# Rotary partners from swapped weight columns, centred value weights, and every fourth head's exponentials from PSUM

## The chip, the cores and the metric

The kernel runs on one core of a Trainium2 chip. Its time is the device time of one execution in microseconds. Three runs of the kernel before the change gave a median of 19321.17 us (19318.22 to 19327.21). The core has five engines that run side by side, each working through its own list of instructions in order: PE (matrix products, which land in PSUM), DVE (elementwise operations and reductions), ACT (tabulated functions and copies), POOL, and SP, which here only starts DMA transfers. An engine that reaches an instruction whose input isn't ready stands still, and everything behind that instruction waits too.

## What is computed

Thirty-two audio signals of 160,000 samples become 32 sequences of 313 frames of 512 samples. Then, cut to what matters:

```python
h = frames @ dct.T                                   # 313 x 512 per sequence
# attention on layernorm(h): 8 heads of width 64
Q = xpos(X @ W_Q); K = xpos(X @ W_K); V = X @ W_V    # xpos: x*cos + rot(x)*sin
#   rot(x)[2i] = -x[2i+1];  rot(x)[2i+1] = x[2i]
p = softmax(Q @ K.T) * gamma_h ** abs(n - m)
Y = p @ V
Yn = (Y - mean(Y)) * rsqrt(var(Y) + 1e-5)            # per head, over its 64 columns
h = h + (silu(X @ W_G) * (Yn * gn_weight + gn_bias)) @ W_O
# feed-forward on x = layernorm(h), 256 neurons
theta = x[..., None, :] / (1 + abs(W)) + B           # 512 angles for each neuron and frame
s, c = sin, cos of theta, rounded to 4096 steps of the circle
out = sum(c * attn_cos) @ proj_cos.T + sum(s * attn_sin) @ proj_sin.T
h = h + silu(out)
```

The sines are the bulk of it: for each neuron, ACT evaluates one sine and one cosine of every element of every frame.

## The kernel before

**Work and stages.** Sequences are taken in eight groups of four (a "quad"). `attention` handles one sequence at a time: DCT, layernorm, projections, heads, norm, output projection. `ffn` handles a quad at once, one neuron after another; its data lie with the 512 features over 4 x 128 partitions and 4 x 313 frames along the free dimension. For each neuron DVE makes the index of the sine (four affine operations at L556, a mask at L563), then the index of the cosine (L568, L574); ACT evaluates both (L581, 5008 elements a partition each, into one of three `trig` buffers); PE sums them over features with a table of weights, `hot` (L591). There are two pairs of index buffers, so DVE can run about one neuron ahead of ACT.

The first quad's attention runs before any FFN work, two sequences side by side in two sets of buffers, A and B; each has its own PSUM tile W of four banks. After that only set A is left, and the attention of the next quad is laid between the neurons of the current one. The eighth quad's FFN has no attention beside it.

**What sets the order.** Nothing is issued as the Python code runs. Each operation is added to a `Plan` with a key (when it is due, in half neurons), an engine, an estimated duration, and what it reads and writes; PSUM is named by bank there (`banks`). `emit` simulates the engines with these durations: each engine takes the ready operation with the lowest key, and the instructions are issued in that order. The chip then runs every engine's list in exactly this order, with semaphores between engines that the tile framework derives from the tiles themselves.

**The lines that the change touches.** `rows` and `columns` load weights of 256 KB into a ring of three buffers (`load`, L203) and multiply: `rows` gives three row blocks in banks 0 to 2 (L274), `columns` one block of 128 output columns in one bank with four matmuls (L288). For each pair of heads g (L326 to L345), two column blocks give q and k in banks 0 and 1; ACT copies both to `raw` (L209); DVE multiplies them by the cosine table (L334); PE multiplies `raw` by a constant matrix `rot`, which swaps neighbours and sets signs, into banks 2 and 3 (L339); DVE multiplies by the sine table (L343) and adds (L344). For each head, PE makes the scores in banks 0 to 2 (L353), DVE takes each row's maximum (L361) and writes scores minus maximum to `prob` (L364). After four heads, ACT takes their exponentials in place, one call per head and row block, with row sums (L372), between two changes of its table. For each of the four heads, PE transposes (L390), DVE multiplies by the decay (L402), and PE multiplies by the values (L408) into bank 3. After every second head DVE takes the mean of each head's 64 columns (L424, L425) and writes the difference to `xn` (L429). The norm follows (L439 to L459), with the square on ACT and the inverse square root on POOL.

Of the kernel before, what the change touches and what calls it, by code (L numbers as in the profile page):

```python
# [12 lines left out]
F32 = mybir.dt.float32  # L13
I32 = mybir.dt.int32
I16 = mybir.dt.int16
AF = mybir.ActivationFunctionType
# [110 lines left out]
def tile_audio_tower(ctx: ExitStack, tc: tile.TileContext, t: dict, out: bass.AP):  # L127
# [20 lines left out]

    xT_d = dram.tile([P, NC4, T], F32, name="xT_d")
    sums_d = dram.tile([2, P, 2, T], F32, name="sums_d")  # L150
    h_d = dram.tile([n_quads, QUAD, S, HOP], F32, name="h_d")

    class Buffers:


        def __init__(self, name, pool, psum):
            self.name = name
            self.n_ring = 0

# [12 lines left out]
            self.raw = sb("raw", 2, S)  # L172
            self.prob = sb("prob", NB, NT, S)
            self.probT = sb("probT", NT, S)
            wide = self.prob.rearrange("p a b s -> p (a b s)")
            self.sq = wide[:, : NT * HOP].rearrange("p (i d) -> p i d", d=HOP)
            self.hres = self.sq
            self.aff = wide[:, NT * HOP : NT * HOP + NC4 * S].rearrange("p (c s) -> p c s", s=S)
            self.mx = [sb(f"mx{i}", NT) for i in range(2)]
            for key in ("sm", "gm", "gv", "gr", "gu"):  # L180
                setattr(self, key, sb(key, NT, H))
            self.st = sb("st", NT, nc.vector.BN_STATS_DIM)
            self.mv = sb("mv", NT, 2)
            for key in ("lv", "lr", "lu"):
                setattr(self, key, sb(key, NT))
            self.W = psum.tile([P, 4, 512], F32, name=f"{name}_W")

            self.y = self.W[:, 3, : NT * 2 * DH].rearrange("p (i d) -> p i d", d=2 * DH)
# [7 lines left out]
        def every(self, key, n):  # L196
            return [self.k(key, x) for x in range(n)]

        def load(self, plan, key, src):

            i = self.n_ring % N_RING
            self.n_ring += 1
            plan.add(key, "SP", DMA_NS, lambda: nc.sync.dma_start(self.ring[i], src), (),  # L203
                     (self.k("ring", i),))
            return i

    def copy(plan, key, eng, n, dst, src, r, w):
        if eng == "ACT":
            plan.add(key, eng, 220 + 0.833 * n, lambda: nc.scalar.copy(dst, src), r, w)  # L209
        else:  # L210
            plan.add(key, eng, 160 + 1.042 * n, lambda: nc.vector.tensor_copy(dst, src), r, w)
# [52 lines left out]
                    )  # L264
            plan.add(key, "PE", 800, go, x.every("xn", NT), x.banks(c))

    def rows(plan, key, x, lhsT, src, r, order=range(NT)):

        for c in range(NC4):
            k = x.load(plan, key, src[c])  # L270
# [21 lines left out]
    def attention(plan, keys, q, b, x):  # L292
# [4 lines left out]
        def step(n=1.0):  # L297
            done[0] += n
            return keys(done[0] / 139.0)
# [9 lines left out]
        copy(plan, step(), ENG_XNT, NC4 * S, x.xnT, x.W[:, :, :S], x.banks(0, 1, 2, 3), (x.k("xnT"),))  # L309


        rows(plan, step(7), x, x.xnT, t["wv"], (x.k("xnT"),), range(NT - 1, -1, -1))
        copy(plan, step(), ENG_V, NT * HOP, x.v[:N], W3, x.banks(0, 1, 2), (x.k("v"),))
        plan.add(step(0), "POOL", 500, lambda: nc.gpsimd.memset(x.v[0:1, : NT - 1, :], 0.0), (),
                 (x.k("v"),))
# [9 lines left out]
        for hb in range(H // NB):  # L325
            for g in range(hb * NB // 2, (hb + 1) * NB // 2):  # L326
                key = step(4)
                qk = x.qk[g % 2]
                kq = x.k("qk", g % 2)
                columns(plan, key, x, 0, t["wq"][g])  # L330
                columns(plan, key, x, 1, t["wk"][g])
                copy(plan, key, "ACT", 2 * S, x.raw, x.W[:, 0:2, :S], x.banks(0, 1), (x.k("raw"),))
                plan.add(key, "DVE", 810,
                         lambda qk=qk: nc.vector.tensor_tensor(qk, x.W[:, 0:2, :S], cos_qk, ALU.mult),  # L334
                         x.banks(0, 1), (kq,))

                def go():
                    for i in range(2):
                        nc.tensor.matmul(x.W[:, 2 + i, :S], rot, x.raw[:, i, :], start=True, stop=True)  # L339
                plan.add(key, "PE", 1100, go, (x.k("raw"),), x.banks(2, 3))  # L340

                def turned(qk=qk):
                    nc.vector.tensor_tensor(x.raw, x.W[:, 2:4, :S], sin_qk, ALU.mult)  # L343
                    nc.vector.tensor_tensor(qk, qk, x.raw, ALU.add)  # L344
                plan.add(key, "DVE", 1640, turned, x.banks(2, 3), (x.k("raw"), kq))  # L345
            for hd in range(hb * NB, (hb + 1) * NB):
# [3 lines left out]
                for i in range(NT):  # L350
# [9 lines left out]
                plan.add(key, "DVE", 1150,  # L360
                         lambda m=m: nc.vector.tensor_reduce(m[:N], x.W[:N, :NT, :S], AX.X, ALU.max),  # L361
                         x.banks(0, 1, 2), (x.k("mx", hd % 2),))
                plan.add(key, "DVE", 1150,
                         lambda m=m, a=a: nc.vector.tensor_tensor(  # L364
                             x.prob[:N, a], x.W[:N, :NT, :S],
                             m[:N].unsqueeze(2).to_broadcast((N, NT, S)), ALU.subtract),
                         (x.k("mx", hd % 2), *x.banks(0, 1, 2)), (x.k("prob", a),))

            def exps(hb=hb):
                for a in range(NB):  # L370
                    for i in range(NT):
                        nc.scalar.activation(  # L372
                            x.prob[:N, a, i, :], x.prob[:N, a, i, :], AF.Exp,
                            accum_out=x.sm[:N, i, hb * NB + a : hb * NB + a + 1],
                        )

                nc.scalar.activation(x.lu[:1, 0:1], x.lu[:1, 0:1], AF.Silu)
            plan.add(step(), "ACT", 8700, exps, (), [*probs, x.k("sm", hb), x.k("lu")])
            for hd in range(hb * NB, (hb + 1) * NB):
                key = step(5)  # L380
                a, d = hd % NB, hd % 2
# [33 lines left out]
                if hd % 2 == 0:  # L415
                    continue

                key = step()
                h0 = hd - 1
                y4 = x.y[:N].rearrange("p i (h e) -> p i h e", e=DH)  # L420
                m = x.gm[:N, :, h0 : h0 + 2]

                def means(m=m, y4=y4):
                    nc.vector.tensor_reduce(m, y4, AX.X, ALU.add)  # L424
                    nc.vector.tensor_scalar(m, m, 1.0 / DH, None, ALU.mult)  # L425
                plan.add(key, "DVE", 750, means, x.banks(3), (x.k("gm", h0),))
                plan.add(
                    key, "DVE", 560,
                    lambda h0=h0, m=m, y4=y4: nc.vector.tensor_tensor(  # L429
                        x.xn[:N, :, h0 * DH : (h0 + 2) * DH].rearrange("p i (h e) -> p i h e", e=DH),  # L430
                        y4, m.unsqueeze(3).to_broadcast((N, NT, 2, DH)), ALU.subtract),
                    (*x.banks(3), x.k("gm", h0)), xns,
                )


# [182 lines left out]
        nc.sync.dma_start(tl, t[key])  # L618
        return tl

    rot = load("rot", P)
    cos_qk = load("cos_qk", 2, S)
    sin_qk = load("sin_qk", 2, S)
    gnw = load("gnw", NC4)
# [4 lines left out]
    def affine(plan, key, x):  # L629
# [11 lines left out]
        def go():  # L641
# [11 lines left out]
        plan.add(key, "DVE", 14000, go, (), ["f", *x.every("prob", NB)])  # L653

    SLOTS = 2.0 * NF
    plan = Plan()
    A = Buffers("a", const, psum)
    affine(plan, -2000.0, A)
# [1 line left out]
    inner = ExitStack()  # L660
    B = Buffers("b", inner.enter_context(tc.tile_pool(name="early", bufs=1)),
                inner.enter_context(tc.tile_pool(name="early_psum", bufs=1, space=PSUM)))
    for b in range(QUAD):
        attention(plan, lambda x: -1000.0 + b // 2 + x, 0, b, (A, B)[b % 2])

# [22 lines left out]
def _constants(S):  # L688
# [18 lines left out]
    for fn, val in (("sin", sin), ("cos", cos)):  # L707
        both = []
        for z in (zeta, (f(1.0) / zeta).astype(f)):
            r = np.repeat(val * z, 2, axis=-1).T  # L710
            both.append(np.concatenate([r, r], 0))
        c[f"{fn}_qk"] = np.ascontiguousarray(np.stack(both, 1))

    rot = np.zeros((P, P), f)
    even = np.arange(0, P, 2)
    rot[even + 1, even] = -1.0
    rot[even, even + 1] = 1.0
    c["rot"] = rot

    lo, hi = f(math.log(1.0 / 32)), f(math.log(1.0 / 512))  # L720
    step = np.arange(H, dtype=f) / f(H - 1)
# [29 lines left out]
def _layout(x, W_Q, W_K, W_V, W_G, W_O, gn_weight, gn_bias, W, B_param, attn_cos, attn_sin, pc, psn):  # L751
# [6 lines left out]
    def heads(w):  # L758
        return w.transpose(1, 0, 2).reshape(HOP, H * DH)

    a["wq"], a["wk"], a["wg"] = _columns(heads(W_Q)), _columns(heads(W_K)), _columns(W_G)
    a["wv"], a["wo"] = _rows(heads(W_V)), _rows(W_O)
    a["gnw"] = np.ascontiguousarray(gn_weight.reshape(NC4, P).T)
    a["gnb"] = np.ascontiguousarray(gn_bias.reshape(NC4, P).T)
# [37 lines left out]
```

## Time and profile before

| | |
|---|---|
| median of three runs | 19321.17 us (19318.22 to 19327.21) |
| the profiled execution | 19307.72 us |
| its span, first to last instruction | 19305.9 us |
| ACT busy | 18394.0 us (95%) |
| DVE busy | 17893.9 us (93%) |
| PE busy (matmuls) | 14624.3 us (76%) |
| POOL busy | 583.0 us (3%) |
| first sine on ACT | 619.3 us after the start |
| one cycle of a quad, FFN and attention | 2348.4 us |

All times below are microseconds unless marked ns. A line of a group gives the source line, engine, operation, output and inputs, shape and count, then busy time, mean ns of one, and the engine's idle time just before with what ended it. Busy times of a group leave out overlap of neighbours, so they can be below count times mean. An engine's idle time costs only where that engine, at that moment, sets the pace.

### The profile page before, as it was taken

Reading aid. Unit: us, or ns where it says so; the run is one execution under the profiler, and the core shown is the slowest. Engines: PE = TensorE matmul, PEld = TensorE weight load, DVE = VectorE, ACT = ScalarE, POOL = GpSimd, SP = SyncE. Lnnn points to the kernel's source line nnn. Section 1 sums busy time; section 2 is a strip of 40 time slices with the busy share of each in tenths; the row PEclk is TensorE's granted clock in tenths of the full one; section 3 lists DMA queues with packets and bytes.
Section 4 is the critical chain, followed back from the end, with each engine's and each line's share of the span. In section 5 each row is a group of like instructions: output and inputs, shape, how many; then the busy total and the mean of one; then the engine's idle time right before and its main releaser. Section 6 shows DMA issues by size and latency. Waiting matters only on the chain.

```text
span 19305.9 us, 332892 instructions
## 1 busy us (share of the span) xinstructions
PE 14624.3 (76%) x147328; PEld 6443.6 (33%) x147328; DVE 17893.9 (93%) x17258; ACT 18394.0 (95%) x6179; POOL 583.0 (3%) x1222
## 2 busy tenths in 40 slices
PE   8777778777787777777777777777777777766666
PEld 5333333333333333333333333233333333322222
DVE  4899999999999999999999999999999999999997
ACT  1799999999999999999999999999999999999998
POOL 0000000000000000000000000000000000000000
PEclk7899989999899998999989999899998999999988
DMA  2111111111111111111111111111111111110001
GB/s 81 41 36 38 36 31 59 37 37 37 35 53 39 36 37 46 43 38 37 37 57 31 36 37 38 56 37 34 35 38 60 35 36 36 36 48 17 18 18 36
DMA packets 418068, 759.10 MB, mean 39 GB/s; under 512 B 50000, under 2 KB 99280, under 8 KB 416624
## 3 DMA queue, kind: packets, MB, share of 16 engines
q1 hardware_dynamic: 416624, 737.80, 12.6%
q8 instruction: 1156, 18.94, 0.4%
q14 instruction: 288, 2.36, 0.0%
HBM read 655.55 MB, written 82.05 MB: 38 GB/s over the span
## 4 chain that ended last, share of the span: by engine, by line
DVE 37%; ACT 34%; PE 15%; issue 11%; POOL 2%; DMA 0%; DVEq 0%; ACTq 0%; SPq 0%; POOLq 0%
ACT trig L581 32%; DVE ix L556 14%; PE pa L591 9%; DVE ix L563 6%; DVE ix L568 6%; DVE ix L574 5%; PE a_W L274 2%; PE a_W L288 1%; DVE a_prob L364 1%; DVE a_mx L361 1%; ACT a_prob L372 1%; PE a_W L353 0%; POOL a_lu L225 0%; PE a_W L408 0%; DVE a_st L237 0%
## 5 line engine op out<-in xcount | busy, mean ns | idle before, releaser
L581 ACT ACTIVATE trig<-ix 128x5008 f32<-128x5008 int16 x4096 | 17539.1, 4366 | 280.2 <-DVE ix L563 202.5
L591 PE MATMUL pa<-trig,hot 128*32 128x313 f32 x131072 | 10641.9, 471 | 4110.8 <-ACT trig L581 4089.2
L591 PEld LDWEIGHTS pa<-trig,hot 128*32 128x32 f32 x131072 | 4127.4, 117 | 10249.9 <-ACT trig L581 5925.4
L556 DVE TENSOR_SCALAR ix<-xT,f_scale,f_bias 128x1252 int16<-128x1252 f32 x8192 | 7099.1, 927 | 273.3 <-ACT trig L581 266.7
L568 DVE TENSOR_SCALAR ix<-ix 128x5008 int16<-128x5008 int16 x2048 | 3005.6, 1468 | 202.2 <-ACT trig L581 16.1
L574 DVE TENSOR_SCALAR ix<-ix 128x5008 int16<-128x5008 int16 x2048 | 3004.6, 1467 | 63.8
L563 DVE TENSOR_SCALAR ix<-ix 128x5008 int16<-128x5008 int16 x2048 | 2998.7, 1464 | 67.3
L288 PE MATMUL a_W<-a_xnT,a_ring 128*128 128x313 f32 x2880 | 834.2, 435 | 0.0
L274 PE MATMUL a_W<-a_ring,a_a 128*105 128x512 f32 x1488 | 696.8, 609 | 24.4 <-DMA a_ring<-in_dct 12.9
L353 PE MATMUL a_W<-a_qk 64*105 64x313 f32 x1440 | 522.3, 482 | 232.6 <-DVE a_prob L364 182.7
L288 PEld LDWEIGHTS a_W<-a_xnT,a_ring 128*128 128x128 f32 x2880 | 529.0, 190 | 282.5 <-issue 72.9
L408 PEld LDWEIGHTS a_W<-a_v,a_probT 105*105 105x105 f32 x4320 | 484.1, 189 | 277.4 <-issue 212.2
L408 PE MATMUL a_W<-a_v,a_probT 105*105 105x64 f32 x4320 | 547.9, 278 | 11.3 <-DVE a_probT L402 8.3
L274 PE MATMUL a_W<-a_ring,a_gate 128*105 128x512 f32 x720 | 370.3, 633 | 62.5 <-DVE a_gate L471 62.5
L353 PEld LDWEIGHTS a_W<-a_qk 64*105 64x105 f32 x1440 | 226.9, 179 | 524.0 <-DVE a_prob L364 270.7
L274 PEld LDWEIGHTS a_W<-a_ring,a_a 128*105 128x105 f32 x1488 | 240.4, 173 | 416.7 <-issue 384.4
L372 ACT ACTIVATE a_prob<-a_prob 105x313 f32<-105x313 f32 x720 | 322.9, 450 | 52.6 <-DVE a_prob L364 52.0
L225 POOL TENSOR_TENSOR a_gu<-a_gr 105x24 f32<-105x24 f32 x90 | 48.7, 541 | 10254.2 <-DVE a_gr L219 10249.5
L274 PE MATMUL a_W<-a_ring,a_xnT 128*105 128x512 f32 x720 | 351.5, 612 | 3.1 <-ACT a_xnT L209 3.1
L261 PE MATMUL a_W<-ident,a_xn 105*128 105x105 f32 x1080 | 185.4, 301 | 189.4 <-DVE a_xn L249 96.0
L390 PE MATMUL a_W<-ident,a_prob 105*105 105x105 f32 x2160 | 321.6, 283 | 8.2 <-DVE a_xn L429 5.3
L361 DVE TENSOR_REDUCE a_mx<-a_W 105x3 f32<-105x939 f32 x240 | 271.0, 1129 | 41.0 <-PE a_W L353 40.9
(137 smaller groups left out, 4368.2 us busy)
## 6 DMA issues: line engine op xcount, KB each, us to landing
hot<-in_hot SPq DMA_DIRECT2D x1024, 256.0 KB
a_dec<-in_decay SPq DMA_DIRECT2D x240, 260.5 KB
a_ring<-in_proj SPq DMA_DIRECT2D x128, 256.0 KB
a_ring<-in_dct SPq DMA_DIRECT2D x120, 256.0 KB
a_ring<-in_wv SPq DMA_DIRECT2D x120, 256.0 KB
a_ring<-in_wg SPq DMA_DIRECT2D x120, 256.0 KB
a_ring<-in_wq SPq DMA_DIRECT2D x120, 256.0 KB
a_ring<-in_wk SPq DMA_DIRECT2D x120, 256.0 KB
```

The source lines that it names most:

```text
L274: lambda c=c, i=i, k=k, to=to: nc.tensor.matmul(x.W[:N, to, :], lhsT[:, c, ROW0[i] : ROW0[i] + N], x.ring[k], start=(c == 0), stop=(c == N ...
L288: nc.tensor.matmul(x.W[:, bank, :S], w[:, c, :], x.xnT[:, c, :], start=(c == 0), stop=(c == NC4 - 1))
L353: lambda i=i, qk=qk, r0=r0: nc.tensor.matmul(x.W[:N, i, :S], qk[r0 : r0 + DH, 0, ROW0[i] : ROW0[i] + N], qk[r0 : r0 + DH, 1, :], start=Tru ...
L361: lambda m=m: nc.vector.tensor_reduce(m[:N], x.W[:N, :NT, :S], AX.X, ALU.max),
L372: nc.scalar.activation(x.prob[:N, a, i, :], x.prob[:N, a, i, :], AF.Exp, accum_out=x.sm[:N, i, hb * NB + a : hb * NB + a + 1],)
L408: nc.tensor.matmul(x.y[:N, i, (hd % 2) * DH : (hd % 2 + 1) * DH], x.probT[:N, jj, ROW0[i] : ROW0[i] + N], x.v[:N, jj, hd * DH : (hd + 1) * ...
L556: nc.vector.tensor_scalar(now["ix", x][:, c, :], now["xT", c], f_scale[:, c, n : n + 1], f_bias[:, c, n : n + 1], ALU.mult, ALU.add)
L563: nc.vector.tensor_scalar(now["ix", x], now["ix", x], LUT - 1, LUT // 2, ALU.bitwise_and, ALU.bitwise_xor)
L568: nc.vector.tensor_scalar(new("ix", y, [P, NC4, T], I16, bufs=N_IX), now["ix", x], float(LUT // 4), None, ALU.add)
L574: nc.vector.tensor_scalar(now["ix", x], now["ix", x], LUT - 1, None, ALU.bitwise_and)
L581: nc.scalar.activation(new("trig", w, [P, NC4, T], bufs=N_TRIG), now["ix", x], AF.Sin, bias=-PI32, scale=ANG)
L591: nc.tensor.matmul(now["pa", p][b * 32 : b * 32 + 32, :S], now["hot", z][:, n % 2, c, k, :], now["trig", w][:, c, b * S : (b + 1) * S], st ...
```

## The change

Four edits. The rotary partners of q and k come from two more column blocks, with weights whose neighbouring columns are swapped (`wq_s`, `wk_s`, prepared with the other weights); the sign moves into the sine table, and the copy to `raw` and the matrix `rot` go. A new function `centre` runs once at the start: it loads the value weights into B's `prob`, subtracts from each head's 64 columns their mean, and stores the result in DRAM as `wv_d`, which every sequence then loads in place of `wv`; the values, and so the head outputs, have zero mean, and the mean on DVE goes. For the last head of every four, DVE no longer writes scores minus maximum: it negates the maximum, and ACT's exponential reads the scores from PSUM with the negated maximum as its bias. The tile `gm` goes.

```diff
+    wv_d = dram.tile([NC4, P, HOP], F32, name="wv_d")
...
-        rows(plan, step(7), x, x.xnT, t["wv"], (x.k("xnT"),), range(NT - 1, -1, -1))
+        rows(plan, step(7), x, x.xnT, wv_d, (x.k("xnT"),), range(NT - 1, -1, -1),
+             ("wv_d",))
...
                 columns(plan, key, x, 0, t["wq"][g])
                 columns(plan, key, x, 1, t["wk"][g])
-                copy(plan, key, "ACT", 2 * S, x.raw, x.W[:, 0:2, :S], x.banks(0, 1), (x.k("raw"),))
+                columns(plan, key, x, 2, t["wq_s"][g])
+                columns(plan, key, x, 3, t["wk_s"][g])
...
-                def go():
-                    for i in range(2):
-                        nc.tensor.matmul(x.W[:, 2 + i, :S], rot, x.raw[:, i, :], start=True, stop=True)
-                plan.add(key, "PE", 1100, go, (x.k("raw"),), x.banks(2, 3))
...
+                if a == NB - 1:
+                    plan.add(key, "DVE", 100,
+                             lambda m=m: nc.vector.tensor_scalar(m[:N], m[:N], -1.0, None, ALU.mult),
+                             (), (x.k("mx", hd % 2),))
+                    continue
...
-            def exps(hb=hb):
+            def exps(hb=hb, m=m):
                 for a in range(NB):
                     for i in range(NT):
+                        last = a == NB - 1
                         nc.scalar.activation(
-                            x.prob[:N, a, i, :], x.prob[:N, a, i, :], AF.Exp,
+                            x.prob[:N, a, i, :],
+                            x.W[:N, i, :S] if last else x.prob[:N, a, i, :], AF.Exp,
+                            bias=m[:N, i : i + 1] if last else 0.0,
                             accum_out=x.sm[:N, i, hb * NB + a : hb * NB + a + 1],
                         )
...
-            plan.add(step(), "ACT", 8700, exps, (), [*probs, x.k("sm", hb), x.k("lu")])
+            plan.add(step(), "ACT", 8700, exps, (x.k("mx", 1), *x.banks(0, 1, 2)),
+                     [*probs, x.k("sm", hb), x.k("lu")])
...
-                def means(m=m, y4=y4):
-                    nc.vector.tensor_reduce(m, y4, AX.X, ALU.add)
-                    nc.vector.tensor_scalar(m, m, 1.0 / DH, None, ALU.mult)
-                plan.add(key, "DVE", 750, means, x.banks(3), (x.k("gm", h0),))
                 plan.add(
-                    key, "DVE", 560,
-                    lambda h0=h0, m=m, y4=y4: nc.vector.tensor_tensor(
-                        x.xn[:N, :, h0 * DH : (h0 + 2) * DH].rearrange("p i (h e) -> p i h e", e=DH),
-                        y4, m.unsqueeze(3).to_broadcast((N, NT, 2, DH)), ALU.subtract),
-                    (*x.banks(3), x.k("gm", h0)), xns,
+                    step(), "DVE", 560,
+                    lambda h0=h0: nc.vector.tensor_copy(
+                        x.xn[:N, :, h0 * DH : (h0 + 2) * DH], x.y[:N]),
+                    x.banks(3), xns,
                 )
...
-    rot = load("rot", P)
...
+    def centre(plan, key, x):
+        wide = x.prob.rearrange("p a b s -> p (a b s)")
+        w = wide[:, : NC4 * HOP].rearrange("p (c d) -> p c d", d=HOP)
+        w3 = wide[:, : NC4 * HOP].rearrange("p (n e) -> p n e", e=DH)
+        m = wide[:, NC4 * HOP : NC4 * HOP + NC4 * H]
+        probs = x.every("prob", NB)
+        def fetch():
+            for c in range(NC4):
+                nc.sync.dma_start(w[:, c, :], t["wv"][c])
+        plan.add(key, "SP", NC4 * DMA_NS, fetch, (), probs)
+        def go():
+            nc.vector.tensor_reduce(m, w3, AX.X, ALU.add)
+            nc.vector.tensor_scalar(m, m, 1.0 / DH, None, ALU.mult)
+            nc.vector.tensor_tensor(
+                w3, w3, m.unsqueeze(2).to_broadcast((P, NC4 * H, DH)), ALU.subtract)
+        plan.add(key, "DVE", 5000, go, (), probs)
+        def store():
+            for c in range(NC4):
+                nc.sync.dma_start(wv_d[c], w[:, c, :])
+        plan.add(key, "SP", NC4 * DMA_NS, store, probs, ("wv_d",))
...
+    centre(plan, -1999.0, B)
...
+            if fn == "sin":
+                r = r * np.tile(np.array([-1, 1], f), half)[:, None]
```

More of the change, by code (lines that the diff above doesn't have):

```diff
@@ L179, in __init__ @@
             self.mx = [sb(f"mx{i}", NT) for i in range(2)]
-            for key in ("sm", "gm", "gv", "gr", "gu"):
+            for key in ("sm", "gv", "gr", "gu"):
                 setattr(self, key, sb(key, NT, H))
@@ L197, in every, with load @@
             return [self.k(key, x) for x in range(n)]
-        def load(self, plan, key, src):
+        def load(self, plan, key, src, r=()):
             i = self.n_ring % N_RING
             self.n_ring += 1
-            plan.add(key, "SP", DMA_NS, lambda: nc.sync.dma_start(self.ring[i], src), (),
+            plan.add(key, "SP", DMA_NS, lambda: nc.sync.dma_start(self.ring[i], src), r,
                      (self.k("ring", i),))
@@ L265, in transposed, with rows @@
             plan.add(key, "PE", 800, go, x.every("xn", NT), x.banks(c))
-    def rows(plan, key, x, lhsT, src, r, order=range(NT)):
+    def rows(plan, key, x, lhsT, src, r, order=range(NT), src_r=()):
         for c in range(NC4):
-            k = x.load(plan, key, src[c])
+            k = x.load(plan, key, src[c], src_r)
             for to, i in enumerate(order):
@@ L416, in attention @@
                     continue
-                key = step()
                 h0 = hd - 1
-                y4 = x.y[:N].rearrange("p i (h e) -> p i h e", e=DH)
-                m = x.gm[:N, :, h0 : h0 + 2]
-                def means(m=m, y4=y4):
-                    nc.vector.tensor_reduce(m, y4, AX.X, ALU.add)
-                    nc.vector.tensor_scalar(m, m, 1.0 / DH, None, ALU.mult)
-                plan.add(key, "DVE", 750, means, x.banks(3), (x.k("gm", h0),))
-                plan.add(
-                    key, "DVE", 560,
-                    lambda h0=h0, m=m, y4=y4: nc.vector.tensor_tensor(
-                        x.xn[:N, :, h0 * DH : (h0 + 2) * DH].rearrange("p i (h e) -> p i h e", e=DH),
-                        y4, m.unsqueeze(3).to_broadcast((N, NT, 2, DH)), ALU.subtract),
-                    (*x.banks(3), x.k("gm", h0)), xns,
+                plan.add(
+                    step(), "DVE", 560,
+                    lambda h0=h0: nc.vector.tensor_copy(
+                        x.xn[:N, :, h0 * DH : (h0 + 2) * DH], x.y[:N]),
+                    x.banks(3), xns,
                 )
@@ L710, in _constants @@
             r = np.repeat(val * z, 2, axis=-1).T
+            if fn == "sin":
+                r = r * np.tile(np.array([-1, 1], f), half)[:, None]
             both.append(np.concatenate([r, r], 0))
         c[f"{fn}_qk"] = np.ascontiguousarray(np.stack(both, 1))
[L714 to L718, printed above, removed]
     lo, hi = f(math.log(1.0 / 32)), f(math.log(1.0 / 512))
@@ L761, in _layout @@
     a["wq"], a["wk"], a["wg"] = _columns(heads(W_Q)), _columns(heads(W_K)), _columns(W_G)
+    a["wq_s"], a["wk_s"] = (
+        _columns(heads(w).reshape(HOP, -1, 2)[:, :, ::-1].reshape(HOP, -1)) for w in (W_Q, W_K))
     a["wv"], a["wo"] = _rows(heads(W_V)), _rows(W_O)
```

## The prediction

> **What bounds the kernel now.** I read the busy time by stage first, because the page's averages (ACT 95%, DVE 93%, PE 76%) mix a start-up with eight repetitions of one cycle. The first table below is the start-up (the first four sequences, without FFN work); its columns are the stretch, its length, the busy time of PE, PEld, DVE, ACT and POOL, the granted TensorE clock, and the DMA share and rate. The row below it is one whole steady cycle of 2348.4 us, in which the FFN of four sequences runs with the attention of the next four laid between.
>
> ```profile
> 50.00:100.00 50.00, 50.00 (x171) 31.55 (x170) 7.29 (x9) 8.79 (x9) 1.88 (x2) 1.00 0.37 111
> 150.00:200.00 50.00, 48.50 (x200) 36.31 (x200) 23.76 (x30) 6.91 (x17) 0.00 (x0) 0.77 0.20 59
> ...
> 450.00:500.00 50.00, 48.51 (x163) 31.62 (x163) 28.82 (x33) 8.36 (x23) 0.00 (x0) 0.77 0.16 48
> ...
> 5315.40:7663.80 2348.40, 1809.01 (x18420) 792.52 (x18416) 2230.96 (x2157) 2298.51 (x773) 77.82 (x152) 0.92 0.13 40
> ```
>
> Two regimes. Up to the first sine at 619.3 us, PE is the bound (48 to 50 of each 50 us where the projections and heads run) and ACT is nearly idle. After that ACT is busy 2298.5 of 2348.4 us and DVE 2231; PE has 539 us of room. There are seven cycles with attention (28 sequences), then one without.
>
> Next the waits inside that cycle: who waited for whom, total us, times, longest.
>
> ```profile
> ACT trig L581 <- DVE ix L563: 28.3, 17, 4.3
> ...
> DVE a_raw L343 <- PE a_W L288: 14.1, 7, 3.8
> ...
> ACT trig L581 <- DVE ix L574: 8.4, 6, 2.0
> ...
> DVE a_mx L361 <- PE a_W L353: 5.1, 3, 2.9
> ...
> ACT trig L581 <- PE pa L591: 2.6, 3, 0.9
> ACT a_raw L209 <- DVE a_qk L334: 2.6, 2, 1.3
> ```
>
> ACT idles 50 us per cycle, and 39.3 of them (28.3 + 8.4 + 2.6) are DVE coming late. Asked in stretches of 20 us over one sequence (5400 to 5990), the waits separate: up to 5560 DVE waits for ACT at nearly every index block (0.5 us each), so ACT sets the pace; from 5580 to 5950 DVE never waits for ACT, and ACT waits for DVE four times (3.3, 3.4, 0.7, 2.0 us). So **DVE is the bound from the second rotary pair through scores and value products to the norm**, which is where the change removes DVE work.
>
> Third, the groups of one cycle (four sequences): busy us, mean ns.
>
> ```profile
> L372 ACT ACTIVATE a_prob<-a_prob 105x313 f32<-105x313 f32 x96 | 43.0, 450 | 0.1
> ...
> L209 ACT COPY a_raw<-a_W 128x626 f32<-128x626 f32 x16 | 10.6, 665 | 2.6 <-DVE a_qk L334 2.6
> ...
> L364 DVE TENSOR_TENSOR a_prob<-a_W,a_mx 105x939 f32<-105x939 f32 x32 | 36.3, 1136 | 1.1
> ...
> L429 DVE TENSOR_TENSOR a_xn<-a_W,a_gm 105x384 f32<-105x384 f32 x16 | 8.9, 558 | 0.5
> ...
> L424 DVE TENSOR_REDUCE a_gm<-a_W 105x6 f32<-105x384 f32 x16 | 8.8, 551 | 0.5 <-PE a_W L288 0.5
> ...
> L425 DVE TENSOR_SCALAR a_gm<-a_gm 105x6 f32<-105x6 f32 x16 | 2.7, 170 | 0.6
> ...
> L288 PE MATMUL a_W<-a_xnT,a_ring 128*128 128x313 f32 x384 | 111.1, 434 | 0.0
> ...
> L339 PE MATMUL a_W<-a_raw,rot 128*128 128x313 f32 x64 | 21.4, 456 | 0.0
> ```
>
> Last, one look at how the PSUM tile W is ordered (timeline, end of an early sequence; lines as start, duration, engine):
>
> ```profile
> 260.59 1.31 PE L261 MATMUL a_W<-ident,a_xn 105*128 105x105 f32 x6 [7.35 <-DVE a_xn L456]
> ...
> 261.94 0.60 DVE L466 TENSOR_SCALAR a_prob<-a_W,gnw,gnb 128x313 f32<-128x313 f32 x1 [1.11 <-PE a_W L261]
> ...
> 262.60 0.79 PE L261 MATMUL a_W<-ident,a_xn 105*128 105x105 f32 x3 [0.70 <-DVE a_prob L466]
> ```
>
> L466 reads bank 0, yet starts only after the transposes of banks 0 and 1; bank 2's transposes start only after that read. W's four banks behave as one object: a reader waits for the last PE write laid out before it, and the next write waits for that reader. L343 waiting on L288, which writes another bank, is the same thing.
>
> **The change, part by part.**
>
> *Rotary partners from PE.* Per pair of heads ACT loses one copy: 0.665 us, some 0.57 net, since a sine starts 4.28 us after the one before though it lasts 4.37 (overlap 0.09). Four per sequence: 2.3 us of ACT. PE gains two column blocks and loses two rotation matmuls: a block costs 111.1/48 = 2.31 us, the rotation 21.4/16 = 1.34, so +3.28 us per pair and +13.1 us per sequence. In the steady cycle that lies in the 539 us of room (52 used; PE 77% to 79%). The cover is thin only while two pairs run: 4 blocks (9.2 us) beside the FFN's matmuls (about 2.3 us of every 4.28). ACT has three sine buffers, so a PE late by over two sines stalls ACT; today that costs 2.6 us per cycle, and I add 0.3 us per sequence. In the **start-up nothing covers it**: blocks follow each other there every 2.115 us (two from 79.58 to 83.81), a rotation takes 1.06 (85.92 to 86.98), so 16 pairs x (4.23 - 1.06) = **+51 us**. Eight more 256 KB loads per sequence go through SP's queue and the ring of three; the DMA share is 0.13 in the cycle. In the start-up a block every 2.1 us needs 124 GB/s, and the first row above shows 111 in such a stretch, so this is near but not over what is seen. Hot-table loads queue behind ring loads; no PE wait on them shows today, and I charge nothing (one late table would stall PE, and then ACT, by a few us).
>
> *Where the DVE stall goes.* L343's wait (14.1/4 = 3.5 us per sequence) need not vanish. Blocks 0 to 3 now follow each other on PE. If block 2 is laid out before the cosine multiply L334, that read of banks 0 and 1 waits for it, and the sine multiply waits likewise for the next pair's first block. Behind it on DVE queue the index operations that ACT needs. From both sides: 0, if an FFN matmul falls between or DVE arrives late anyway, up to 2.3 us (one block) per pair, 9 us per sequence; below nothing, if L343's 3.5 go too. I take +1.0 us per sequence, because the nearest row, L343's own wait, hit 7 of 16 pairs, and DVE is mostly late there itself.
>
> Here a rule of the Trainium skill stands against the row. "PSUM — Partial Sum Buffer" (Terms) forbids two engines only the same bank, in AWS's words "no two of the three engines may access the same bank within the same partition in one cycle". By that, L334 on banks 0 and 1 would run beside block 2, the 1.0 us would be 0, and the total 28 us better. The row above shows waits across banks, so I keep the 1.0.
>
> *Centred value weights.* Removed per two heads: L424 and L425, from 161.43 to 162.23 in the timeline, 0.80 us; four times 3.2 us per sequence. The subtraction L429 (558 ns) becomes a copy of as many elements; by the PSUM copy L603 (478 ns for 313 elements, so about 552 for 384) it costs the same. Once, at the start: four loads ahead of the first frames on SP (0.47 us of issue each, 1 MB of traffic), less one load that goes: PE's first matmul, at 12.86 us, starts about 2.5 us later. DVE adds a reduction (1.75 x 2048/1536 = 2.3), 0.2 and a subtraction (2.3), after the FFN constants that end at 22.7; stored by about 32 us, read by PE from 38.5. It is hidden; without that cover, about 5 us once.
>
> *Every fourth head straight from PSUM.* DVE loses L364 twice per sequence (1.06 us start to next start) and gains a negation of 3 columns like L425 (0.21): 1.7 us. On ACT six exponentials read PSUM (about 0.04 us less, by the 1536-element rows: copy from PSUM 1426 ns, square from SBUF 1466) with a bias that is a tensor. The row of today shows no such bias: 450 ns is 313 elements at 0.833 plus 189. The skill's "ScalarE: Activation LUTs" (What ACT_TABLE_LOAD costs) puts about 93 ns on each pointer operand: +0.3 us per sequence with it, -0.2 without; I take +0.3 on ACT. The transposes of the batch's first head must now wait for the last exponential, but PE idles 8.9 us behind the exponentials anyway (pa matmul at 5634.91, waiting for a sine).
>
> **The sum.** DVE per sequence -3.2 - 1.7 = -4.9 us, all in the stretch where DVE is the bound. ACT there has 9.4 us of waits and gives up 2.0 itself, so it doesn't cap this. Plus 1.0 (stalls) and 0.3 (sine buffers): -3.6 us; x 28 = -101. ACT's own saving is not added: where DVE is the bound it becomes waiting. Start-up: +51 + 2.5 - 4 (shorter chains of DVE work between PE's steps, mostly behind the other buffer) = +49. Net -52: the profiled run of 19307.7 (span 19305.9, 1.8 around it) becomes about 19256; the median of the runs is 13.5 above that run, so about **19269**.
>
> **Rivals.**
> *More than forecast:* L343's wait goes without a successor. 4.9 + 3.5 = 8.4 us x 28 = 235, less 49: 19135. For it: the ACT copy between two PE steps is gone. Against: blocks still follow one another in one tile. I give it 0.2, mostly as half of it (about 19190).
> *Slower:* the DVE stall moves to L334. One block's wait per pair, met half-way (1.15 us x 4 = 4.6), eats the 4.9, and the start-up's 49 stays: 19370; met in full 19500. It decides above 3.1 us of new stalls per sequence (4.9 - 49/28). For it: whole-tile waits; against: DVE arrives late where it is the bound. 0.15.
> *No change:* PE's extra blocks hold sine buffers; 3 us per sequence of ACT waits on L591 bring it to about 19320. Today only 2.6 us per cycle. 0.15.
> The forecast, with its own range 19230 to 19300, keeps 0.5.
>
> **Numbers.** A measurement tells 0.2%, 39 us, from no change. Faster: most of 0.5 + 0.2 = 0.66; same 0.18; slower 0.16. The range 19160 to 19375 leaves out the full first rival and the slower one beyond its mean.
>
> **What would show it.** First sine at about 668 us instead of 619. Cycle of about 2334 us instead of 2348.4. L424, L425, L339 and the raw copies gone; L364 x24 per cycle. "ACT trig waits for DVE ix" down from 37 to some 25 us, DVE waits on PE at L334 and L343 together near 18. I am wrong if the cycle stays above 2341 (stalls at L334, or sine waits on PE), or if the first sine comes before 650 us.

## The result, and the profile after

The changed kernel takes **19194.72 us** (median of four runs, 19181.59 to 19200.94) against 19319.69 for the kernel before, measured beside it: a ratio of 0.9935, interval 0.9918 to 0.9952. The forecast was 19269, faster, with a range of 19160 to 19375. The direction held and the time lies in the range, but the gain is 125 us where 52 were forecast. The profiled execution spans 19199.2 us, 106.7 less than before.

By stage, in the same view as before (length, then busy PE, PEld, DVE, ACT, POOL, the clock, DMA share and rate). Up to the first sine PE is busy 579.9 of 679.7 us; before, it was 530.0 of 619.3. One whole cycle of the changed kernel:

```profile
5328.70:7653.20 2324.50, 1844.65 (x18608) 829.17 (x18604) 2212.80 (x2125) 2289.51 (x757) 77.58 (x152) 0.93 0.15 44
```

The cycle went from 2348.4 to 2324.5 us: ACT is busy 9.0 us less and idle 15 us less (35 instead of 50). DVE is busy 18 us less but idle almost as much as before (111.7, was 117.4). The sines, by the view of their source line, start later and end earlier:

```profile
L581 ACT ACTIVATE trig<-ix x4096: 4354/4364/4408, 679.7 to 19126.1; 128x5008 f32<-128x5008 int16 x196
```

The first came at 619.3 us before (60.4 later now), the last at 19234.6. From first to last it was 18615.3 us and is 18446.4. That is the measure I use below for the steady part: -168.9 us, or **-24.1 per cycle** over the seven cycles with attention. With the start-up's +60.4 it makes -108.5, close to the -106.7 of the span. The whole steady part, first before and then after the change, in the same view:

```profile
619.00:19239.00 18620.00, 14047.07 (x145240) 6071.52 (x145240) 17623.33 (x16889) 18273.28 (x5915) 547.87 (x1064) 0.91 0.12 38
```

```profile
679.60:19131.00 18451.40, 14340.21 (x146592) 6327.00 (x146596) 17498.49 (x16664) 18212.33 (x5803) 546.22 (x1064) 0.92 0.14 41
```

ACT is busy 61 us less in it (18212.3, was 18273.3), and it waits 181.0 us for DVE where it waited 284.2, which is 103 us less. These two make up nearly all of the 168.9.

Who waited for whom in the one cycle:

```profile
DVE ix L556 <- ACT trig L581: 31.2, 49, 3.5
...
ACT trig L581 <- DVE ix L563: 17.7, 12, 4.2
...
PE a_W L289 <- DVE a_qk L338: 8.8, 9, 1.6
...
ACT trig L581 <- DVE ix L574: 7.0, 4, 2.0
...
PE a_W L289 <- DVE a_raw L342: 3.3, 5, 1.3
...
ACT trig L581 <- PE pa L591: 2.6, 3, 0.9
...
DVE a_xn L430 <- PE a_W L289: 2.2, 2, 1.3
...
DVE a_qk L338 <- PE a_W L289: 1.9, 3, 0.9
```

DVE's waits for PE around the rotary and the first maximum (14.1 + 5.1 us) are almost gone: the cosine multiply (L338 now) waits 1.9, the copy of the head outputs 2.2, the sine multiply not at all. ACT waits 24.7 us for DVE instead of 39.3. And DVE waits for ACT at the index operations 31.2 us where it was 21.3: part of the time that DVE saves, it now spends waiting. W is still one tile, but now PE waits: 12.1 us per cycle (8.8 + 3.3) before a column block (L289), for DVE's two multiplies; before the change no matmul of these blocks (L288) waited for DVE. PE has that time to give: it is busy 1844.7 of 2324.5 us. The cost of the new exponential also shows:

```profile
L378 ACT ACTIVATE a_prob<-a_prob 105x313 f32<-105x313 f32 x72 | 32.3, 451 | 0.1
...
L378 ACT ACTIVATE a_prob<-a_W,a_mx 105x313 f32<-105x313 f32 x24 | 12.0, 505 | 0.0
```

From PSUM with a tensor as bias one takes 54 ns more.

### The profile page after: what moved, and what is told of

Its sections match the earlier page's. It is cut to its first block, busy times and chain, and to the rows that moved or that the text cites. A ratio compares the mean times of both kernels' runs of the same rounds, so it can differ in the third digit from the quotient of the medians.

```text
span 19199.2 us, 336270 instructions
## 1 busy us (share of the span) xinstructions
PE 14967.9 (78%) x148864; PEld 6732.7 (35%) x148864; DVE 17754.5 (92%) x17005; ACT 18323.5 (95%) x6051; POOL 581.0 (3%) x1222
## 4 chain that ended last, share of the span: by engine, by line
ACT 36%; DVE 33%; PE 17%; issue 11%; POOL 3%; DMA 0%; DVEq 0%; ACTq 0%; SPq 0%; POOLq 0%
ACT trig L581 34%; DVE ix L556 13%; PE pa L591 11%; DVE ix L563 5%; DVE ix L568 5%; DVE ix L574 5%; PE a_W L275 2%; PE a_W L289 2%; ACT a_prob L378 1%; DVE a_mx L360 1%; PE a_W L417 1%; PE a_W L352 1%; DVE a_prob L369 1%; POOL a_lu L226 1%; DVE a_st L238 0%
## 5 line engine op out<-in xcount | busy, mean ns | idle before, releaser
L289 PE MATMUL a_W<-a_xnT,a_ring 128*128 128x313 f32 x4800 | 1402.1, 437 | 92.2 <-DVE a_qk L338 66.6
L289 PEld LDWEIGHTS a_W<-a_xnT,a_ring 128*128 128x128 f32 x4800 | 873.3, 190 | 618.3 <-issue 156.1
L352 PE MATMUL a_W<-a_qk 64*105 64x313 f32 x1440 | 481.2, 459 | 100.8 <-DVE a_prob L369 75.9
L399 PEld LDWEIGHTS a_W<-ident,a_prob 105*105 105x105 f32 x2160 | 282.0, 205 | 393.8 <-ACT a_prob L378 260.9
L378 ACT ACTIVATE a_prob<-a_prob 105x313 f32<-105x313 f32 x540 | 242.6, 451 | 67.2 <-DVE a_prob L369 66.5
```

The lines of the kernel that those rows point to most:

```text
L289: nc.tensor.matmul(x.W[:, bank, :S], w[:, c, :], x.xnT[:, c, :], start=(c == 0), stop=(c == NC4 - 1))
L352: lambda i=i, qk=qk, r0=r0: nc.tensor.matmul(x.W[:N, i, :S], qk[r0 : r0 + DH, 0, ROW0[i] : ROW0[i] + N], qk[r0 : r0 + DH, 1, :], start=Tru ...
L378: nc.scalar.activation(x.prob[:N, a, i, :], x.W[:N, i, :S] if last else x.prob[:N, a, i, :], AF.Exp, bias=m[:N, i : i + 1] if last else 0. ...
L399: nc.tensor.transpose(x.W[:N, jj, ROW0[i] : ROW0[i] + N], x.prob[:N, a, i, ROW0[j] : ROW0[j] + N], ident[:N, :N],)
```

## The experiments

Each time is a median and each ratio is to the kernel before, measured beside it. "Steady" is the time from the first to the last sine, from one profile each; its difference, divided by seven, is the figure per cycle. Worked out instead from the medians, less the shift of the first sine, the figures per cycle come out up to 2.4 us different (-26.5 for the whole change, -6.5 for the change without the rotary). Differences smaller than that are not told apart here.

### One part alone: the rotary

Built from the kernel before:

```diff
-                copy(plan, key, "ACT", 2 * S, x.raw, x.W[:, 0:2, :S], x.banks(0, 1), (x.k("raw"),))
+                columns(plan, key, x, 2, t["wq_s"][g])
+                columns(plan, key, x, 3, t["wk_s"][g])
...
-                        nc.tensor.matmul(x.W[:, 2 + i, :S], rot, x.raw[:, i, :], start=True, stop=True)
```

> Only the rotary part of the change. Theory (stall): what it brings in the cycle is that DVE stops waiting for PE behind W's next write, 19.2 us per cycle at the sine multiply and the maximum; those waits fall below 5, the cycle goes from 2348.4 to 2333-2340 and the first sine comes at about 670 us; time about 19295. Rival (ACT): it brings ACT's 16 copies of 0.57 us, so 2339, with DVE still waiting 10 us or more for PE. Rival (nothing): the cycle stays at 2348, all the gain is DVE work removed elsewhere, and the start-up makes it 19370.

Measured: 19232.30 us, ratio 0.9962 (0.9948 to 0.9976); first sine at 680.4 us; steady 18475.7, -19.9 per cycle. Waits of ACT and DVE in one cycle of 2327.95 us:

```profile
ACT trig L578 <- DVE ix L560: 21.7, 14, 4.2
...
DVE a_qk L336 <- PE a_W L288: 1.7, 2, 0.9
```

The rotary part alone brings five sixths of the steady gain (19.9 of 24.1), and DVE's waits for W around the rotary and the maximum fall to 1.7 us. The cycle is below even the first theory's 2333 to 2340. The rotary part also carries the whole loss of the start-up.

### The change without the rotary

> The change without its rotary part: centred weights and every fourth head from PSUM, the old copy and matrix kept. Theory (stall): DVE loses 4.9 us per sequence, the sine multiply's wait of about 14 us per cycle stays; cycle 2330-2335, first sine at about 627 us (2.5 for the transfers and 5.7 for the order at the start). Rival (ACT sets the pace after all): cycle above 2340, since ACT's list isn't shorter. Rival (the rotary part brings nothing): cycle 2324 as in the changed kernel.

The edit puts the copy to `raw`, the matrix and the unsigned sine table back into the changed kernel.

Measured: 19275.04 us, ratio 0.9980 (0.9972 to 0.9989); first sine at 625.1; steady 18581.4, **-4.8 per cycle**. Of the three expectations only the rival that called ACT the pace-setter (a cycle above 2340) holds. In a cycle of about 2345 us:

```profile
ACT trig L584 <- DVE ix L566: 22.9, 14, 4.2
ACT trig L584 <- DVE ix L577: 7.4, 5, 2.0
...
DVE ix L559 <- ACT trig L584: 28.8, 45, 3.5
...
DVE a_raw L345 <- PE a_W L289: 10.4, 6, 3.6
...
DVE a_mx L363 <- PE a_W L355: 7.7, 4, 3.2
```

DVE is busy 2215 us per cycle instead of 2231, yet the cycle hardly moves: DVE waits longer for ACT (28.8) and for PE at the maximum (7.7, was 5.1). PE's matmuls took 18.7 us more in this cycle, at a granted clock of 0.91 (0.92 before), so a little of this can be PE's. By either measure, 4.8 or 6.5, the forecast's main term, 4.9 us of DVE work per sequence (19.6 per cycle) counted in full, is refuted.

### The old rotary with PSUM of its own

```diff
-    N_IX, N_TRIG, N_HOT, N_PA = 4, 3, 2, 4
+    N_IX, N_TRIG, N_HOT, N_PA = 4, 3, 2, 2
...
+                kr = (x.k("R"),) if q else x.banks(2, 3)
...
-                        nc.tensor.matmul(x.W[:, 2 + i, :S], rot, x.raw[:, i, :], start=True, stop=True)
...
+                        nc.tensor.matmul(R[:, i, :S], rot, x.raw[:, i, :], start=True, stop=True)
...
+        A.R = pools["bank"].tile([P, 2, 512], F32, name="a_R")
```

> The kernel before the change, with the rotation's product in a PSUM tile of its own (two banks, taken from the four of the FFN sums) from the second quad on; nothing else moves. Theory (W is ordered as one object): the sine multiply no longer waits for the next column block, 14.1 us per cycle become under 2, and the cycle falls by 5 to 12 us from 2348.4. Rival (the wait is PE being late, whatever the tile): it stays above 8 us and the cycle within 3 us. The FFN sums with two banks may cost 1-2 us per cycle.

Measured: 19202.17 us, ratio 0.9942 (0.9928 to 0.9957); first sine at 621.5; steady 18507.1, **-15.5 per cycle**, beyond the 5 to 12 expected. One cycle of 2331.8 us; the sine multiply no longer appears among the waits:

```profile
ACT trig L585 <- DVE ix L567: 17.9, 11, 4.2
ACT trig L585 <- DVE ix L578: 7.9, 6, 2.0
...
DVE a_mx L365 <- PE a_W L357: 0.9, 2, 0.6
```

What has moved is the PSUM tile of one product, with what the planner makes of it; the FFN sums have two banks instead of four. ACT's busy time is that of before within 1.1 us (2297.38), so what went is idle time: 15.5 us of it, for 16.7 us of DVE's waits for W (14.1 + 5.1 + 0.5 at the mean before, 0.9 + 2.1 now). So those waits were worth nearly their length.

The timelines show what the waits were. Before, the rotation (L339) is done at 5568.62, but the sine multiply starts only when the next pair's block, which goes to bank 0, is done at 5570.73:

```profile
5567.30 1.32 PE L339 MATMUL a_W<-a_raw,rot 128*128 128x313 f32 x4
...
5568.46 2.27 PE L288 MATMUL a_W<-a_xnT,a_ring 128*128 128x313 f32 x8
...
5570.84 0.81 DVE L343 TENSOR_TENSOR a_raw<-a_W,sin_qk 128x626 f32<-128x626 f32 x1 [2.04 <-PE a_W L288]
```

With a tile of its own it starts 0.11 us after the rotation, in the middle of that block:

```profile
5541.42 1.32 PE L342 MATMUL a_R<-a_raw,rot 128*128 128x313 f32 x4
...
5542.58 2.27 PE L288 MATMUL a_W<-a_xnT,a_ring 128*128 128x313 f32 x8
5542.85 0.81 DVE L347 TENSOR_TENSOR a_raw<-a_R,sin_qk 128x626 f32<-128x626 f32 x1
```

In this program, then, W was ordered as one object. With no other part of the change, this kernel comes within 8 us of the whole change's median, since its start-up stays short. Both together were not run.

### ACT's copy put back without its chain

```diff
+                copy(plan, key, "ACT", 2 * S, x.a5[:, 0:2, :], x.xnT[:, 0:2, :], (x.k("xnT"), *x.banks(1)), (x.k("a5"),))
```

> The changed kernel with one more copy on ACT per pair of heads, as large as the one removed (128x626), from xnT into the buffer a5, where nobody reads it: ACT's load is back, the chain through ACT and W is not. Theory (ACT's own time counts in full, beside its waits: the rotary part alone gave 20.4 us per cycle, 9.3 of them ACT busy time): the cycle grows by 7-10 us over 2324.4, to 2331-2334. Rival (DVE sets the pace in the rotary and score stretch, so ACT has room there): 0-4 us.

Measured: 19244.55 us, ratio 0.9967 (0.9955 to 0.9978); first sine at 673.7; steady 18494.1, +6.8 per cycle over the changed kernel. That is three quarters of the copies' 9.1 us (by the medians 8.0), at the edge of the theory's 7 to 10 and well over the rival's 0 to 4. Before the rotary part was measured alone, I had held these two the other way round, with 0 to 4 as the theory. ACT's own time counts mostly in full, and the forecast had counted none of it.

### Every fourth head from PSUM alone

> Only every fourth head from PSUM. Theory (lead: DVE time counts only where its lead of one neuron is used up, which is the scores): 8 x 0.85 us less DVE in the scores of a cycle, 1.3 more ACT: cycle 4-6 us below 2348.4, about all of what centring and this gave together (4.9). Rival (both parts share the 4.9 by their DVE time, 12.8 to 6.8): 1-2 us. Start-up within 2 us of 619.

The edit puts only the negated maximum and the exponential from W into the kernel before.

Measured: 19292.83 us, ratio 0.9992 (0.9984 to 1.0001); first sine at 611.7; steady 18606.8, **-1.2 per cycle**. This is the rival's size, and it is not told apart from no change: 6.8 us of DVE work gone brought next to nothing, with 1.3 us of ACT work added. By difference, centring would bring 3.6 of the 4.8; it was not run alone. The start-up was expected within 2 us of 619 and is 7.6 shorter.

### The same DVE work in three places

Three kernels put the two instructions of the removed means back into the changed kernel, on data that lie ready, with a result nobody uses:

```diff
+                def more(x=x, h0=hd - 1):
+                    m = x.gu[:N, :, h0 : h0 + 2]
+                    nc.vector.tensor_reduce(
+                        m, x.v[:N, :, : 2 * DH].rearrange("p i (h e) -> p i h e", e=DH), AX.X, ALU.add)
+                    nc.vector.tensor_scalar(m, m, 1.0 / DH, None, ALU.mult)
```

once after every second head's maximum, once after every second head's products, and once twice in a row after the first rotary pair of every four heads.

> The changed kernel with the DVE work of the removed means put back, on other data (a reduction of 105x384 and a small multiply, 0.8 us, four times per sequence; nobody reads the result), placed in the scores after the maximum of every second head. Theory (lead): it counts nearly in full there, the cycle grows by 9-13 us over 2324.4. Rival (only the sum of DVE work counts): the same as with this work beside the products.

> The same DVE work as in the kernel with it in the scores, placed where the means were, after the value products of every second head. Theory (lead): DVE has time to give there, the cycle grows by 0-3 us over 2324.4. Rival (only the sum of DVE work counts): by the same as with the work in the scores, 9-13 us if DVE is the bound.

> The changed kernel with the same DVE work as in the two kernels before (12.8 us per cycle), in lumps of 1.6 us, one after the first rotary pair of every four heads, where DVE used to stand waiting for PE. From the first to the last sine, per cycle: those two kernels gave +2.4 and +4.3. Theory (lumps ahead of the scores count, since DVE is one neuron ahead at most and regains 0.7 us per neuron): +8 or more. Rival (any DVE time counts by a fifth to a third): +2 to +5.

The expectations took this as 12.8 us of DVE per cycle in each place. In the traces it is less, because the instructions close up with their neighbours: from start to start a pair takes 0.66 us beside the products and 0.73 in the lump, and beside the scores 0.12 of its 0.66 falls into a gap that is there anyway. The second column has what this makes per cycle.

| where | DVE time added per cycle | steady, per cycle over the changed kernel | time, us | ratio to before (interval) |
|---|---|---|---|---|
| beside the scores, one pair at a time | 8.6 | +4.3 | 19211.88 | 0.9953 (0.9938 to 0.9967) |
| beside the products, one pair at a time | 10.6 | +2.4 | 19211.88 | 0.9951 (0.9936 to 0.9966) |
| before the scores, two pairs at a time | 11.6 | +14.1 | 19305.99 | 0.9994 (0.9986 to 1.0003) |

The first theory of the lead failed: the scores are not a place where DVE time counts in full (about half of it did). The first two rows, 4.3 and 2.4, are not told apart. The third is: the same instructions in lumps, put where DVE used to stand waiting for PE, cost 14.1 us per cycle, at least as much as they last, and take back most of the gain. Lump and place were changed at once, so which of the two decides is open. The waits show where the time went. In 2350 us, a little over a cycle, ACT waits for DVE 36.0 us instead of 24.7:

```profile
ACT trig L590 <- DVE ix L572: 27.2, 18, 4.3
ACT trig L590 <- DVE ix L583: 8.8, 7, 2.0
```

Shown is the price of each placement. The explanation is argued, not shown, though it fits all three: DVE's lead of about one neuron absorbs short pieces, and DVE regains an estimated 0.7 us per neuron (two sines start 8.56 us apart, and one neuron's index operations take 7.87 us of DVE, both from the groups of a cycle), while a lump just ahead of the scores arrives when the next bursts of DVE work follow at once. The kernels also differ in the order that the planner made around the added work.

### The start-up

```diff
+                if q:
+                    columns(plan, key, x, 2, t["wq_s"][g])
+                    columns(plan, key, x, 3, t["wk_s"][g])
+                else:
+                    copy(plan, key, "ACT", 2 * S, x.raw, x.W[:, 0:2, :S], x.banks(0, 1), (x.k("raw"),))
...
+                if not q:
+                    plan.add(key, "PE", 1100, go, (x.k("raw"),), x.banks(2, 3))
```

> The changed kernel, with the rotary partners of the first quad made as before (copy on ACT, product with a matrix, now without signs, since the sine table has them) and swapped columns from the second quad on. Theory (the start-up is PE's: 16 pairs x 3.17 us): first sine 51 us earlier, 625-632 us, cycles as in the changed kernel (2324-2325), time 19140-19150. Rival (the start-up loss is the order and the transfers): first sine above 660.

```diff
-    affine(plan, -2000.0, A)
+    affine(plan, -999.85, A)
```

> The changed kernel with the FFN's constants (two loads, 14 us of DVE) due after the first sequence's layernorm instead of first of all. Theory (the change's centring adds 2.5 us of transfers ahead of the first frames and 5.7 us by moving a normalisation behind DVE's constants): PE's first matmul by 13 us instead of 15.4, first sine 6-10 us earlier than 679.7. Rival (these were hidden behind PE): within 3 us of it.

> Both of these together: first sine at 615-625 us, cycles 2324-2325, time 19130-19142, faster than either kernel.

| kernel | first sine | steady, us | time, us | ratio to before (interval) |
|---|---|---|---|---|
| matrix in the first quad | 616.9 | 18449.5 | 19149.75 | 0.9913 (0.9898 to 0.9928) |
| constants later | 677.2 | 18449.3 | 19204.11 | 0.9941 (0.9926 to 0.9956) |
| both | 608.8 | 18452.2 | 19142.26 | 0.9910 (0.9894 to 0.9927) |

With the matrix in the first quad the start-up is 62.8 us shorter, more than the 51 expected, and the cycles are as in the changed kernel. By the medians it gains 45 us on the changed kernel, and its slowest run (19158.53) is below the fastest of the changed kernel (19181.59): **faster than both**. The constants moved later bring the first sine 2.5 us forward alone (the rival) and 8.1 on top of the other; in the times neither step shows beyond the spread of the runs. The first sine of both, 608.8, is earlier than the 615 to 625 expected. With the constants later PE's first matmul comes at 13.22 us instead of 15.37, so what came back is about the transfers; the 5.7 us that I had put down to the constants did not. In the changed kernel's DVE list, the first normalisation stands behind the second sequence's statistics, which wait for ACT:

```profile
40.41 0.69 DVE L238 BATCH_NORM_STATS2 b_st<-b_h 105x6 f32<-105x512 f32 x1 [7.19 <-ACT b_h L210]
...
42.03 1.43 DVE L250 TENSOR_SCALAR a_xn<-a_h,a_mv,a_lr 105x512 f32<-105x512 f32 x3
```

POOL had finished its input at 36.5 us; before the change this line began at 33.61, ahead of those statistics. With the constants moved, the order is the same, so its cause in the plan wasn't tested.

## Why the forecast was right or wrong

The time lies in the range, but partly by luck: the steady part gained more than forecast and the start-up lost more, and inside the steady part one term was far too large and two were missing. Of the forecast's own signs, ACT's waits for DVE came out as said (24.7 for 25); the cycle (2324.5 for 2334), the first sine (679.7 for 668) and DVE's waits for PE at the rotary (1.9 for 18) did not.

**Right: the start-up's PE cost, with one wait left out.** Two more column blocks per pair at 2.115 us, less a rotation, were to cost 51 us. The rotary part alone cost 61.1 us (680.4 against 619.3); within the change it was 62.8 (679.7 against 616.9). The column blocks of buffer set A up to the first sine, before and with the rotary part alone:

```profile
L288 PE MATMUL a_W<-a_xnT,a_ring 128*128 128x313 f32 x192 | 56.7, 444 | 0.0
```

```profile
L288 PE MATMUL a_W<-a_xnT,a_ring 128*128 128x313 f32 x320 | 90.6, 434 | 3.6 <-DVE a_qk L336 3.6
```

With B's the blocks are busy 69.0 us more, and the rotations that go were 19.9: a net 49.1, close to the 51. On top comes a wait that was not there before: PE waits for the cosine multiply (L336), 3.6 us in A and 4.2 in B. The forecast had charged the meeting of that multiply and the blocks in the cycle, to DVE, and nothing for it in the start-up. The last 4 us are not settled.

**Right: the transfers. Wrong: "it is hidden".** PE's first matmul came at 15.37 us, 2.5 later, as worked out. Centring's DVE work was to be hidden; the first normalisation starts 8.4 us later, 2.5 of them the transfers, the rest the order shown above. The change without the rotary, which contains this and the new exponentials, starts its sines 5.8 us later (625.1). Of the -4 us for shorter chains, the kernel with every fourth head alone showed -7.6 (611.7), but PE's same 1960 matmuls are busy 12.4 us less there, at a mean granted clock of 0.78 instead of 0.75, so what the chains gave stays open. The sum for the start-up was +49 and measured +60.4.

**Wrong: "DVE per sequence -4.9 us, all in the stretch where DVE is the bound".** This was to give 137 us over 28 sequences. The two parts that remove this work gave 4.8 us per cycle without the rotary and 4.2 (24.1 - 19.9) on top of it, some 30 in all. The error was in reading the stretch: that DVE never waited for ACT from 5580 to 5950 was taken to mean that ACT always waited for DVE. The stretch itself, before the change:

```profile
5580.00:5950.00 370.00, 275.40 (x2887) 123.53 (x2879) 351.96 (x347) 360.56 (x138) 12.19 (x25) 0.90 0.10 30
```

ACT, busy 360.6 of 370 us, was fuller there than DVE with 352.0. Its sines waited for DVE only 9.3 us, six times (the prediction's "four times" are four stretches of 20 us). For the rest both ran, with DVE's lead between them.

**Wrong: "ACT's own saving is not added".** The copy put back costs 6.8 us per cycle, 48 us over seven. In the whole steady part ACT is busy 61 us less, and that came on top of the shorter waits; it did not turn into waiting. The steady forecast of -101 us was to be shorter waits alone, and ACT's waits for DVE did fall by 103. That these agree is luck, since the terms inside the 101 were wrong.

**Wrong: the stall, taken as +1.0 us per sequence with 3.5 staying.** Both went: the waits at the rotary and the first maximum fell from 19.2 us per cycle to 1.9, and the kernel with a PSUM tile of its own shows that this wait was worth 15.5 us per cycle, 108 over seven. In the changed kernel it is PE that waits at these places. The forecast's estimate from below had this, as the first rival, with 0.2. That rival's 19135 also kept the 4.9 in full (by the runs 107 us too much) and left out ACT's own saving (48 us). What I feared, the cosine multiply waiting for block 2, costs 1.9 us per cycle.

**The row against the rule.** The Trainium skill's "PSUM — Partial Sum Buffer" (Terms) keeps engines apart by bank; I kept the trace's row, which showed waits across banks of W. The run with a tile of its own confirms the row: the waits belong to the tile as this program orders it. By the rule the stall would have been 0 and the forecast 28 us lower, 19241, nearer to the measured time but for a reason that the rows contradict. Yet deciding for the row misled the size: it named the stall that would go, and I charged one that stayed.

**Right: the exponential's 54 ns**, worked out as 93 for a tensor bias (the Trainium skill's "ScalarE: Activation LUTs", What ACT_TABLE_LOAD costs) less 40 for reading PSUM. The runs show only the sum.

Two sizes were off in opposite ways: 137 us of DVE time became 30, and the rotary in the steady part, forecast as a loss of 36, became a gain of 140. The net of a wrong and an omitted term came out with the right sign.

## What to carry to other kernels

An engine that never waits in a stretch isn't thereby its bound: put a little work on it there, or take a wait away, and see whether the end moves. Where two engines run in step with a small lead, price the long waits and the lumps just ahead of a burst at full length, and work spread in short pieces at a fraction; here the same instructions cost 2.4, 4.3 or 14.1 us per cycle. And cost a change separately for stages with different bounds: doing the rotary one way in the PE-bound start-up and the other way afterwards gives 19150 us.

## What the runs showed that I had not expected

A product moved to a PSUM tile of its own brought 15.5 us per cycle, about as much over the whole kernel (19202 us) as the change with all its parts (19195 us). And the start-up varies beyond its work: with the same column blocks in it, the first sine came between 659.0 and 685.5 us. The start-ups of the kernels with the DVE work beside the scores and in lumps:

```profile
0.00:659.00 659.00, 554.18 (x2152) 361.22 (x2152) 256.32 (x369) 105.41 (x245) 34.82 (x158) 0.82 0.29 91
```

```profile
0.00:685.50 685.50, 585.13 (x2152) 391.57 (x2152) 259.28 (x369) 105.50 (x244) 35.13 (x158) 0.77 0.29 88
```

PE makes the same 2152 matmuls in both, but is busy 31 us longer in the second, where the mean granted clock is 0.77 instead of 0.82. So the spread is in PE's time for the same work, and not in waits. Why the clock differs between two orders of the same matmuls is open.
